# A two-layer graph attention kernel in float32: row loads in fewer, larger transfers, weight loads held back behind VectorE, and a new order at the end of a pass

## The chip, the core and the metric

The kernel runs on one core of a Trainium2 chip. The metric is the device time in microseconds (us) of one execution. The engines are named as the profile names them: PE (TensorE, matmuls) with PEld (its weight loads), DVE (VectorE), ACT (ScalarE), POOL (GpSimd) and SP (SyncE, which here only issues DMAs). Each engine works through its own instructions in order, and waits where a semaphore isn't there yet. All DMAs but two go through SP's one queue, in the order of the program.

## What is computed

There are 128 graphs of 64 nodes with 768 features. The features are normalised, and two layers of graph attention follow; the result is added to the input.

```python
h = jnp.maximum(_layernorm(x, axis=-1), 0.0)
for l in range(L):                               # L = 2
    m_left  = einsum('bsh,oh->bso', h, W_left[l])
    m_right = einsum('bsh,oh->bso', h, W_right[l])
    u_left  = einsum('bih,bjh->bij', h, m_left) / temper
    u_right = einsum('bih,bjh->bij', h, m_right) / temper
    u = u_left * adj_tri + u_left * diag_mask + u_right * swapaxes(adj_tri, 1, 2)
    delta_exp_u = exp(u) * adj
    attention = delta_exp_u / (sum(delta_exp_u, axis=2, keepdims=True) + 1e-10)
    h_lin = einsum('bsh,oh->bso', h, W_lin[l]) + b_lin[l]
    ctx = matmul(attention, h_lin)
    h = relu(_layer_norm(ctx, ln_a[l], ln_b[l]))
return x + h
```

All of it is float32.

## The kernel before

**Tiling and passes.** The tokens are cut into 16 blocks u = 0 to 15 of 8 graphs (512 tokens). Each layer has a pass one (`pass_one`: m_left, m_right, scores, softmax; the attention goes to DRAM) and a pass two (`pass_two`: h_lin, context, normalisation). Pass one takes two blocks at a time: a superblock U = 0 to 7, blocks 2U and 2U + 1.

**Products.** The two 768 x 768 projections of a superblock are done by a scheme of fast matrix multiplication: 29 products (`PRODUCTS`, `NP = 29`) of sums of weight blocks with sums of token blocks, each for the left and the right weights (k = 0, 1). A product writes one of the PSUM banks X, Y, Z (left) or V, right (right); each result is then read out (`read`, line 303) by ACT where an accumulator `m` is new, and added to `m` by DVE otherwise (line 221). One product is 16 matmuls, about 3.43 us. In layer 0's first superblock the weight sums are made as they are needed, on DVE and POOL, and stored to DRAM (`ws`); in all later superblocks they are streamed from there into a ring of eight buffers `wp` (`RINGS = 8`): the load for a product is issued when the product eight before it has released its buffer, about seven products (24 us) ahead.

**Slots.** The order of everything beside the matmuls is written out by hand. A superblock has 4 x 29 = 116 slots, and `run(slot)` is called four times in each product: slots 4i to 4i + 3 belong to product i. `put(slot, f)` lists work for a slot; slots with nothing listed take from the queue `idle`. A list given to `put_all` fills one slot after the other; `None` leaves one empty. What is put in a slot stands at that place in the queue of its engine, SP's included.

**Rows and blocks.** In layer 0, for each block from 2 on, `load_rows` reads the rows of x into SBUF; `transpose_rows` makes the statistics (line 338, DVE), normalises (ACT, line 399) and transposes on DVE (line 414); `store` writes the block to DRAM in four transfers (line 410); and `load_h` brings it back in the layout that the matmuls need (line 373). In `block(n, slot)` the store comes 6 slots after the last transpose, the next block's row load one slot later and `load_h` from 15 slots after the last transpose. The two blocks of a superblock start at the slots in `starts`. Layer 1 does the same from the rows that pass two of layer 0 wrote, without the statistics. A row load is 8 transfers; each takes one graph of 64 rows, as rows 0 to 31 and 32 to 63 side by side on 32 partitions. Blocks 0 and 1 of layer 0 are made by PE transposes in `first`, and lines 674 and 675 store them at slots 54 and 58 of superblock 0, for pass two.

**Held loads.** `HELD` lowers the number of weight loads that SP has issued by the end of a product near a superblock's border, so that other DMAs stand ahead of them in SP's queue. `paced(to, f)` (line 143) writes zeros to one column of a buffer on DVE before the load f into it is issued, so that the load waits for DVE's place.

**Scores.** `scores` (line 464, 192 short matmuls) runs within products 0 and 2 of the next superblock, for the two blocks of the one before, and at the end of pass one for blocks 14 and 15. The generator `chain` is the softmax of a block cut into steps: two with mask products on DVE (line 480), the add (484), the exponential on ACT (486), multiply and sum (488, 490), the division (492 to 494), then transpose (498) and eight stores. `softmax(u)` gives these 15 steps. At the end of pass one, lines 763 to 768 place those of blocks 14 and 15; what goes to `put_all` there runs in the first slots of pass two (two slots to each of its products). Pass two's first products are read out at line 303 by ACT and line 221 by DVE into `hl`.

Of the kernel before, what the change touches and what calls it, by code (L numbers as in the profile page):

```python
# [17 lines left out]
def kernel(  # L18
# [12 lines left out]
    nc = tc.nc  # L31
# [24 lines left out]
    NBB = T // S  # L56
    RINGS = 8
# [5 lines left out]
    none = [None]  # L63

    def put(slot, *fs):
        plan.setdefault(slot, []).extend(fs)

    def put_all(slot, fs, step=1):
        for f in fs:
            if f is not None:  # L70
                put(slot, f)
            slot += step
        return slot
# [50 lines left out]
    NP = len(PRODUCTS)  # L124
# [10 lines left out]
    RING = [wpool.tile([P, 2, K2, D], F32, name=f"wp{i}") for i in range(RINGS)]  # L135
# [4 lines left out]
    def room(n, m):  # L140
        return ROOM[:, n * K2 * D:(n + m) * K2 * D]

    def paced(to, f):

        nc.vector.memset(to, 0.0)
        f()
# [49 lines left out]
    def stream(l, n):  # L196
        nc.sync.dma_start(RING[n % RINGS], WS[l][n % NP])
# [34 lines left out]
    HT, TS = {}, {}  # L232
# [42 lines left out]
    def token_op(l, U, op, eng):  # L275
        i, o, sign, a, b = op
        t = new_ts((l, U, o))
        added(eng, t, sign, tokens(l, U, a), tokens(l, U, b))
        TS.setdefault((l, U), {})[o] = t

    AHEAD_X = 4
    SLOTS = 4 * NP

    def put_token_ops(l, U, part):

        count = {}
        for op in X_OPS:
            n = count[op[0]] = count.get(op[0], 0) + 1
            slot = 4 * (op[0] - AHEAD_X) + n - 1
            if (slot < 0) == (part == "before"):  # L290
                put(slot + (SLOTS if slot < 0 else 0), lambda op=op: token_op(l, U, op, nc.gpsimd))
# [20 lines left out]
    KEPT = [[dram.tile([P, C, T], F32, name=f"h{l}_{u}") for u in range(NB)] for l in range(L)]  # L312
    ROWS = [dram.tile([NBB, S, H], F32, name=f"z_{u}") for u in range(NB)]
# [41 lines left out]
    def blocks_tile(pool):  # L355
        if pool is not None:
            return pool.tile([P, H // 32, Q, 32], F32, name="xb", bufs=1)
        return room(6, 6).rearrange("p (b q j) -> p b q j", q=Q, j=32)

    def load_rows(l, u, pool=None):  # L360

        XR[l, u] = []
        for g in range(2):
            t = rows_tile(pool, g)
            for a in range(4):
                i = 4 * g + a
                src = x[u * NBB + i] if l == 0 else ROWS[u][i]
                nc.sync.dma_start(t[a * 32:(a + 1) * 32], src.rearrange("(k j) h -> j k h", k=2))
            XR[l, u].extend([t[:, 0, :], t[:, 1, :]])

    def load_h(which, l, u):
# [12 lines left out]
    def transpose_rows(l, u, pool=None):  # L384

        xr, todo = XR[l, u], []
        if l == 0:
            mv = stat.tile([P, Q, 2], F32, name="mv0", bufs=2)
            sd = stat.tile([P, Q], F32, name="sd0", bufs=2)
            rs = stat.tile([P, Q], F32, name="rs0", bufs=2)  # L390
            nb = stat.tile([P, Q], F32, name="nb0", bufs=2)

            def scale():
                nc.scalar.activation(sd, mv[:, :, 1], AF.Sqrt, bias=eps_in)
                nc.vector.reciprocal(rs, sd)
                nc.vector.scalar_tensor_tensor(nb, mv[:, :, 0], -1.0, rs, op0=ALU.mult, op1=ALU.mult)

            def norm(q):
                nc.scalar.activation(xr[q], xr[q], AF.Relu, bias=nb[:, q:q + 1], scale=rs[:, q:q + 1])

            norms = [lambda q=q: norm(q) for q in range(Q)]
            stats = [lambda q=q: mean_var(mv[:, q, :], [xr[q][:, :HH], xr[q][:, HH:]]) for q in range(Q)]
            for f in stats + none * (4 * (u < 4)) + [scale] + norms:
                todo.extend([f] + none * (u >= 4))
        xb = blocks_tile(pool)

        def store():
            to = KEPT[l][u].rearrange("(b i) c t -> i c b t", b=4)
            for a in range(4):
                nc.sync.dma_start(to[:, :, :, a * P:(a + 1) * P],  # L410
                                  xb[a * 32:(a + 1) * 32].rearrange("i (c b) q j -> i c b (q j)", b=4))

        for q in range(Q):
            todo.append(lambda q=q: nc.vector.transpose(
                xb[:, :, q, :], xr[q].rearrange("p (b j) -> p b j", j=32)))
            todo.extend(none * (l or u >= 4))
        todo.append(store)
        return todo
# [7 lines left out]
    def pass_one(l, aside):  # L426
        with (tc.tile_pool(name=f"ps_one{l}", bufs=1, space=bass.MemoryType.PSUM) as ps,
# [76 lines left out]
                        nc.sync.dma_start(to[a // 2, a % 2, g], at[a * 32:(a + 1) * 32, g])  # L504

            TURNS = {0: 0, 2: 1}
            HELD = {NP - 2: 1, NP - 1: 2, 0: 3, 1: 4}
            sent = [RINGS - 1 if l else NP + 5]

            def project(U, weights, done):  # L510
# [35 lines left out]
            def streamed(U):  # L546
                def done(i):
                    while sent[0] < min(U * NP + i + RINGS - HELD.get(i, 0), NU * NP):
                        stream(l, sent[0])
                        sent[0] += 1  # L550
                return (lambda i, k: RING[(U * NP + i) % RINGS][:, k]), done

            def first():
# [47 lines left out]
                hts = [new_ht() for _ in range(2)]  # L601
# [66 lines left out]
                for n, (s0, s1, s2, s3) in {4: (3, 4, 5, 8), 5: (6, 7, 8, 12), 6: (13, 14, 15, 19),  # L668
# [2 lines left out]
                    put(s1, lambda n=n: inverse(n))  # L671
                    put(s2, lambda n=n: norm(n))
                    put(s3, lambda n=n: turn(n), lambda n=n: settle(n))
                for n, slot in ((0, 54), (1, 58)):
                    put(slot, lambda n=n: nc.sync.dma_start(KEPT[0][n], hts[n]))
                put(3, lambda: load_rows(0, 2))
                count = {}
                for op in X_OPS:
                    n = count[op[0]] = count.get(op[0], 0) + 1
# [28 lines left out]
            for U in range(NU):  # L708
                if U:
                    weights, done = streamed(U)  # L710
                if l or U:
                    put_token_ops(l, U, "after")
                if U + 1 < NU:
                    def block(n, slot):
                        u = 2 * U + 2 + n
                        *todo, store = transpose_rows(l, u)
                        slot = put_all(slot, todo)
                        put(slot + 6, store)
                        if u + 1 < NB:
                            put(slot + 7, lambda: load_rows(l, u + 1))  # L720
                        slot = max(slot + 15, (92, 103)[n]) if U == 0 and l == 0 else slot + 15
                        put(slot, lambda: load_h(1, l, u))
                        if l:
                            put_all(slot + 20, affine(1, l, u))

                    if l:
                        starts = (6 if U else 20, 48)
                    else:
                        starts = (6, 52) if U else (26, 66)
                    for n, slot in enumerate(starts):  # L730
                        put(slot - 1, lambda n=n, slot=slot: block(n, slot))
                    if U:
                        for n in range(2):
                            steps = softmax(2 * U - 2 + n)
                            slot = put_all(20 + 40 * n if l else (34, 76)[n], steps[:6], 2)
                            slot = put_all(slot, steps[6:] + [lambda n=n: load_adj(2 * U + n)])
                            put(slot + 11, masked(2 * U + n))
                    else:
                        for n in range(2):
                            put((40 if l else 106) + 2 * n, masked(n))  # L740
                    put_token_ops(l, U + 1, "before")
                else:
                    for n in range(2):
                        put(12 + 28 * n, lambda n=n: load_h(2, l, n))
                        put_all(38 + 28 * n, affine(2, l, n))
                    for n in range(2):
                        steps = softmax(2 * U - 2 + n)
                        put_all(put_all(14 + 28 * n, steps[:6], 2), steps[6:])
                    put(40, lambda: load_adj(2 * U))
                    put(54, masked(2 * U))  # L750
                    put(SLOTS - 24, lambda: load_adj(2 * U + 1))
                    put(SLOTS - 10, masked(2 * U + 1))
                    put_sums_t((2, l, 0), 94, 2, 85)
                if U in aside:
                    aside[U]()
                project(U, weights, done)
                assert not plan, sorted(plan)
# [5 lines left out]
            scores(NB - 2, both[0])  # L763
            scores(NB - 1, ps_st.tile([P, 2 * TH], F32, name="Z"))
            one, two = softmax(NB - 2), softmax(NB - 1)
            for f in one[:2] + two[:2] + one[2:] + two[2:4]:
                f()
            put_all(2, two[4:])

    rows = {}  # L770

# [406 lines left out]
```

## Time and profile before

| | us |
|---|---|
| median of 3 runs | 2748.3 (2744.96 to 2752.83) |
| the profiled execution, its own time | 2748.58 |
| its span, first to last instruction | 2746.8 |
| granted TensorE clock | 0.994 |

Shares of 40 equal slices of the span (68.7 us each), each digit in tenths, for PE, DVE and the DMA engines:

```profile
PE   8899999999999999999999999999999999999998
...
DVE  7745755647557433334333645545446475676667
...
DMA  7967867768665334657586967868759524555655
```

The first 13 slices are pass one of layer 0, the next seven its pass two, slices 21 to 33 pass one of layer 1, and the rest its pass two. The DMA engines work hardest in the passes one. The largest DMA issues (count, KB each, median us from issue to landing):

```profile
wp<-ws SPq DMA_DIRECT2D x435, 512.0 KB, 5.4
ht<-h SPq DMA_DIRECT2D x62, 1536.0 KB, 8.8
h<-room SPq DMA_DIRECT2D x112, 384.0 KB, 6.2
...
room<-in_x_dram SPq DMA_DIRECT2D x112, 192.0 KB, 5.2
```

The first is the weight stream, the second `load_h`, the third the store of a block, the last the rows of layer 0 (layer 1's, from `z`, are as many).

### The profile page before, as it was taken

Reading aid. Unit: us, or ns where it says so; the run is one execution under the profiler, and the core shown is the slowest. Engines: PE = TensorE matmul, PEld = TensorE weight load, DVE = VectorE, ACT = ScalarE, POOL = GpSimd, SP = SyncE. Lnnn points to the kernel's source line nnn. Section 1 sums busy time; section 2 is a strip of 40 time slices with the busy share of each in tenths; the row PEclk is TensorE's granted clock in tenths of the full one; section 3 lists DMA queues with packets and bytes.
Section 4 is the critical chain, followed back from the end, with each engine's and each line's share of the span. In section 5 each row is a group of like instructions: output and inputs, shape, how many; then the busy total and the mean of one; then the engine's idle time right before and its main releaser. Section 6 shows DMA issues by size and latency. Waiting matters only on the chain.

```text
span 2746.8 us, 47294 instructions
## 1 busy us (share of the span) xinstructions
PE 2689.4 (98%) x18514; PEld 2309.1 (84%) x18514; DVE 1494.6 (54%) x2458; ACT 828.0 (30%) x1601; POOL 1380.5 (50%) x1071
## 2 busy tenths in 40 slices
PE   8899999999999999999999999999999999999998
PEld 7788888888888788888788888888888888888886
DVE  7745755647557433334333645545446475676667
ACT  4031231321310145445631221211212303444443
POOL 5534244333345766576343324335234185887886
PEclk9999999999999999999999999999999999999999
DMA  7967867768665334657586967868759524555655
GB/s 252 314 225 226 256 218 259 227 202 274 213 226 191 105 127 149 205 155 232 186 279 204 301 196 231 267 188 272 227 186 293 202 76 125 163 168 167 172 164 148
DMA packets 310222, 567.81 MB, mean 207 GB/s; under 512 B 62832, under 2 KB 190064, under 8 KB 301808
## 3 DMA queue, kind: packets, MB, share of 16 engines
q1 hardware_dynamic: 309840, 564.39, 64.7%
q8 instruction: 148, 2.42, 0.4%
q14 instruction: 74, 0.61, 0.1%
q10 hardware_dynamic: 160, 0.39, 0.0%
HBM read 429.40 MB, written 135.27 MB: 206 GB/s over the span
## 4 chain that ended last, share of the span: by engine, by line
PE 93%; POOL 2%; DVE 2%; issue 1%; DMA 1%; ACT 0%; DVEq 0%; POOLq 0%; ACTq 0%; SPq 0%
PE right L522 17%; PE X L1038 12%; PE X L522 10%; PE V L522 10%; PE Y L522 9%; PE Z L522 9%; PE V L1038 8%; PE Y L1038 6%; PE both L464 4%; PE Z L1038 4%; PE aux L846 2%; POOL room L221 1%; PE aux L869 1%; POOL ts L221 1%; PE Y L869 0%
## 5 line engine op out<-in xcount | busy, mean ns | idle before, releaser
L221 POOL TENSOR_TENSOR ts<-ht 128x512 f32<-128x512 f32 x352 | 478.7, 1366 | 176.5 <-PE X L1038 76.8
L221 POOL TENSOR_TENSOR ts<-ht,ts 128x512 f32<-128x512 f32 x192 | 253.2, 1327 | 386.4 <-PE V L522 232.7
L522 PE MATMUL right<-ts,wp 128*128 128x252 f32 (+1 forms) x1632 | 382.1, 377 | 0.0
L522 PEld LDWEIGHTS right<-ts,wp 128*128 128x128 f32 x1632 | 311.1, 191 | 39.1
L473 POOL TENSOR_TENSOR wm<-adj,tri 128x256 f32<-128x256 f32 x60 | 42.8, 736 | 433.0 <-DMA wp<-ws 285.4
L221 DVE TENSOR_TENSOR m<-m,X 128x512 f32<-128x512 f32 x160 | 105.5, 684 | 282.9 <-ACT m L303 199.8
L1038 PE MATMUL X<-room,ts 128*128 128x256 f32 x1024 | 247.2, 383 | 10.1 <-ACT hl L303 9.9
L221 DVE TENSOR_TENSOR m<-m,right 128x504 f32<-128x504 f32 (+1 forms) x304 | 199.2, 672 | 90.3 <-PE right L522 77.1
L522 PE MATMUL Z<-ts,wp 128*128 128x256 f32 x992 | 234.5, 379 | 0.0
L221 POOL TENSOR_TENSOR ts<-ht,ht 128x512 f32<-128x512 f32 x128 | 163.3, 1286 | 138.8 <-PE right L522 93.6
L1038 PEld LDWEIGHTS X<-room,ts 128*128 128x128 f32 x1024 | 193.3, 192 | 42.8 <-issue 12.5
L522 PE MATMUL X<-ts,wp 128*128 128x256 f32 x872 | 208.7, 382 | 1.0 <-DVE wp L221 1.0
L522 PEld LDWEIGHTS Z<-ts,wp 128*128 128x128 f32 x992 | 188.4, 190 | 24.9
L522 PE MATMUL V<-ts,wp 128*128 128x252 f32 (+1 forms) x864 | 201.6, 376 | 0.0
L303 ACT ACTIVATE m<-right 128x504 f32<-128x504 f32 (+1 forms) x64 | 36.1, 590 | 546.7 <-PE both L464 526.7
L522 PEld LDWEIGHTS X<-ts,wp 128*128 128x128 f32 x872 | 165.3, 191 | 24.9 <-issue 1.6
L1038 PE MATMUL Y<-room,ts 128*128 128x256 f32 x768 | 183.6, 381 | 0.0
L522 PEld LDWEIGHTS V<-ts,wp 128*128 128x128 f32 x864 | 164.2, 190 | 20.4
L380 ACT ACTIVATE ht<-ht,b_col,a_col 128x512 f32<-128x512 f32 x192 | 140.8, 803 | 112.6 <-DMA ht<-h 112.6
L1038 PEld LDWEIGHTS Y<-room,ts 128*128 128x128 f32 x768 | 146.9, 191 | 20.9 <-issue 0.6
L221 DVE TENSOR_TENSOR m<-m,Y 128x512 f32<-128x512 f32 x144 | 95.7, 683 | 118.6 <-PE Y L522 107.4
L221 DVE TENSOR_TENSOR hl<-hl,V 128x512 f32<-128x512 f32 (+1 forms) x136 | 89.0, 655 | 129.1 <-PE V L1038 121.5
(221 smaller groups left out, 4866.6 us busy)
## 6 DMA issues: line engine op xcount, KB each, us to landing
wp<-ws SPq DMA_DIRECT2D x435, 512.0 KB, 5.4
ht<-h SPq DMA_DIRECT2D x62, 1536.0 KB, 8.8
h<-room SPq DMA_DIRECT2D x112, 384.0 KB, 6.2
z<-z SPq DMA_DIRECT2D x128, 192.0 KB, 3.1
ws<-wp SPq DMA_DIRECT2D x93, 256.0 KB, 4.3
xr<-in_x_dram SPq DMA_DIRECT2D x120, 192.0 KB, 3.7
out_dram<-xr SPq DMA_DIRECT2D x120, 192.0 KB, 2.6
room<-in_x_dram SPq DMA_DIRECT2D x112, 192.0 KB, 5.2
```

Source lines behind the costliest of these rows:

```text
L221: (eng.tensor_add if sign == "+" else eng.tensor_sub)(o, a, b)
L303: nc.scalar.activation(to(o), p, AF.Copy, scale=1.0 if sign == "+" else -1.0)
L380: nc.scalar.activation(ht, ht, AF.Relu, bias=cols[1][:, c:c + 1], scale=cols[0][:, c:c + 1])
L464: nc.tensor.matmul(p[h * S + e:h * S + e + 32, q, e:e + 95], ht[:, c, b * S + e:b * S + e + 32], mb[:, e:e + 95], start=(c == 0), stop=(c ...
L473: nc.gpsimd.tensor_tensor(wm[:, :, k], adj[:, :, 1 - k], tri[:, k].unsqueeze(1).to_broadcast([P, Q, S]), op=ALU.mult)
L522: nc.tensor.matmul(p[:, g], wk[:, c, g * P:(g + 1) * P], tk[:, c, :].rearrange("p (b s) -> p b s", s=S)[:, :, :ns], start=(new and g == c ...
L846: nc.tensor.matmul(cx[k][i, m, :HH], at[j, q, :], hl[j, q, m * HH:(m + 1) * HH], start=True, stop=True)
L869: nc.tensor.matmul(parts[r, k][n][i], at[j, q, :], hl[j, q, cut], start=True, stop=True)
L1038: nc.tensor.matmul(p[:, n], b[t][:, c, r * P:(r + 1) * P], w[s][:, c, :], start=(i in FIRST and i not in PRELOAD and n == c == 0), stop=(c ...
```

## The change

It has five parts.

- `load_rows` issues 4 transfers in place of 8: for each half of the block (4 graphs) and each half k of the rows one transfer, to all 128 partitions.
- `HELD` is moved by one product. From superblock 1 on, the loads that are let go after product 3 are each tied to DVE by `paced`.
- The stores of blocks 0 and 1 leave superblock 0 and go to slots 20 and 26 of superblock 1.
- In layer 0 the starts move: from (26, 66) to (26, 62) in superblock 0, with two empty slots after the list of each of its blocks, and from (6, 52) to (8, 52) later. The second row load of superblock 0 goes to slot 112.
- At the end of pass one, block 14's add and exponential come before block 15's mask products, and all later steps of block 15 go to pass two's slots from 3 on.

```diff
@@ load_rows
             t = rows_tile(pool, g)
-            for a in range(4):
-                i = 4 * g + a
-                src = x[u * NBB + i] if l == 0 else ROWS[u][i]
-                nc.sync.dma_start(t[a * 32:(a + 1) * 32], src.rearrange("(k j) h -> j k h", k=2))
+            src = x[u * NBB + 4 * g:u * NBB + 4 * g + 4] if l == 0 else ROWS[u][4 * g:4 * g + 4]
+            for k in range(2):
+                nc.sync.dma_start(t[:, k, :], src[:, k * 32:(k + 1) * 32, :])
@@ transpose_rows
             for f in stats + none * (4 * (u < 4)) + [scale] + norms:
                 todo.extend([f] + none * (u >= 4))
+            todo.extend(none * (2 * (u < 4)))
@@ pass_one
-            HELD = {NP - 2: 1, NP - 1: 2, 0: 3, 1: 4}
+            HELD = {NP - 1: 1, 0: 2, 1: 3, 2: 4}
@@ streamed
                     while sent[0] < min(U * NP + i + RINGS - HELD.get(i, 0), NU * NP):
-                        stream(l, sent[0])
+                        if U and i == 3:
+                            paced(RING[sent[0] % RINGS][:, 0, 0, :1], lambda: stream(l, sent[0]))
+                        else:
+                            stream(l, sent[0])
                         sent[0] += 1
@@ first
-                for n, slot in ((0, 54), (1, 58)):
-                    put(slot, lambda n=n: nc.sync.dma_start(KEPT[0][n], hts[n]))
@@ pass_one, the loop over superblocks
+                if l == 0 and U == 1:
+                    for n in range(2):
+                        put(20 + 6 * n, lambda n=n: nc.sync.dma_start(KEPT[0][n], HT[1, 0, n]))
...
-                            put(slot + 7, lambda: load_rows(l, u + 1))
+                            put(SLOTS - 4 if U == 0 and l == 0 and n else slot + 7, lambda: load_rows(l, u + 1))
...
-                        starts = (6, 52) if U else (26, 66)
+                        starts = (8, 52) if U else (26, 62)
@@ pass_one, its end
             one, two = softmax(NB - 2), softmax(NB - 1)
-            for f in one[:2] + two[:2] + one[2:] + two[2:4]:
+            for f in one[:4] + two[:2] + one[4:]:
                 f()
-            put_all(2, two[4:])
+            put_all(3, two[2:])
```

## The prediction

> **What bounds the kernel now.** I read the page's busy line first, then the waits of PE, then the timeline at each wait, and last the DMA windows of an undisturbed superblock.
>
> ```profile
> PE 2689.4 (98%) x18514; PEld 2309.1 (84%) x18514; DVE 1494.6 (54%) x2458; ACT 828.0 (30%) x1601; POOL 1380.5 (50%) x1071
> ```
>
> PE is idle for 2746.8 - 2689.4 = 57.4 us. A change that leaves the matmuls alone can win no more than a part of that; it can lose without limit. PE's waits say where the idle time lies (total, times, longest, in us):
>
> ```profile
> PE both L464 <- issue: 13.0, 9, 2.8
> PE X L1038 <- ACT hl L303: 9.9, 2, 5.1
> PE Y L522 <- DMA wp<-ws: 6.3, 1, 6.3
> PE Y L522 <- DVE room L221: 3.4, 1, 3.4
> ```
>
> The second row is the start of pass two, once per layer; the third is the start of superblock 1 of layer 0. The timeline of each (start, duration, last the idle time before it):
>
> ```profile
> 919.39 0.38 DVE L484 TENSOR_TENSOR wp<-wp 128x256 f32<-128x256 f32 x1
> ...
> 919.81 0.42 ACT L486 ACTIVATE wp<-wp 128x256 f32<-128x256 f32 x1 [4.35 <-DVE wp L145]
> 920.13 0.58 ACT L303 ACTIVATE hl<-X 128x512 f32<-128x512 f32 x1
> ...
> 920.86 3.22 PE L1038 MATMUL X<-room,ts 128*128 128x256 f32 x8 [4.83 <-ACT hl L303]
> ```
> ```profile
> 132.41 3.75 PE L522 MATMUL Y<-ht,wp 128*128 128x256 f32 x8 [6.26 <-DMA wp<-ws]
> ```
>
> ACT's first eviction of pass two stands behind the last block's exponential, and that behind DVE's whole tail of the block before. In steady superblocks (108 us each) PE has no gap, so there only a loss is possible. What carries a steady superblock is the lead of its transfers. SP's queue around one row load, and the windows (share of the DMA engines, GB/s) for row loads and for weight loads:
>
> ```profile
> 392.53 5.20 SPq L410 DMA_DIRECT2D h<-room  x4
> 397.83 6.02 SPq L368 DMA_DIRECT2D room<-in_x_dram  x8
> 403.94 0.84 SPq L197 DMA_DIRECT2D wp<-ws  x2
> ```
> ```profile
> 402.50:406.50 4.00, 4.00 (x21) 3.54 (x20) 3.17 (x5) 1.75 (x4) 3.05 (x3) 1.00 0.96 263
> 408.50:410.50 2.00, 2.00 (x11) 1.78 (x10) 1.24 (x3) 0.00 (x0) 0.00 (x0) 1.00 1.04 411
> ```
>
> Per engine and busy time that is 263/16/0.96 = 17.1 GB/s for rows and 411/16/1.04 = 24.7 GB/s for weights.
>
> [...] In the kernel before the row load's source reads 32 x 2 x 768[...]. The new load's destination is 128 partitions, but its source is 4 blocks x 32 rows x 768[...].
>
> **Part by part.**
>
> *Row loads.* Per block 8 transfers of 192 KB become 4 of 384 KB. SP saves perhaps 3 us of its 6.02. The bytes (1.573 MB) take 1573/16/17.1 = 5.7 us on 16 engines, but on 4 engines 393 KB each: 15.9 us at 24.7 GB/s, 23.0 us at 17.1. [...] I take a value nearer the fast end, 17.6 us. Everything SP issues later queues behind this on these four engines. Steady case, product 10 of the superblock at 355: SP issues the load of product 16 at 395.4 (product 9 begins), the four stores of h to 401 (their packets last some 6.4 us: 1573 KB at the 244 GB/s of 396 to 401, so to about 403.7), then rows, then the load of product 17. Rows end at 421.3; that load adds 524 KB/16/24.7 = 1.3 us and about 1 us to land: 423.6. PE begins product 17 at 422.77. Stall 0.8 us; none (margin 0.9) at the fast end, 6.2 us at the slow end. The next loads have 3.43 us more each and catch up. 11 row loads of layer 0 and 13 of layer 1 stand so: 24 x 0.8 = 19 us, between 0 and 149. On DVE the statistics of the block (L338) wait for the same rows in layer 0; its eviction behind them is due at the same product 17, so this is not added again.
>
> *First superblock.* Two places. The rows of block 2 now sit for 17.6 us on four engines in front of the first stores of weights; weight sums write into buffers only after those stores have landed, first at slot 25 (product 6). Some 5 us. For block 3 the rows' slot goes from 50 to 52 and the statistics from 66 to 62, a lead of 10 slots of 0.86 us = 8.6 us against 13.7:
>
> ```profile
> 67.53 6.06 SPq L368 DMA_DIRECT2D room<-in_x_dram  x8
> ...
> 83.48 1.00 DVE L338 BATCH_NORM_STATS2 st<-room 128x6 f32<-128x384 f32 x2
> ```
>
> On 4 engines the last rows come near 70 + 17.6 + 2 = 90 us, the statistics' place on DVE is near 79: DVE, which PE's evictions and the weight sums stand behind, is held for about 10 us; some 8 reach PE. Together +13, between 0 (rows on 16 engines) and 25.
>
> *Stores of blocks 0 and 1 moved to superblock 1, last row load of superblock 0 at slot 112.* 3.1 MB, 8 us of all engines at 24.7 GB/s each, leave the busy stretch from 72 to 100 us, and 8 row loads no longer stand ahead of the weight stores that the first streamed loads wait for. That removes the 6.26 us stall and the slow first matmuls behind it (3.75 against 1.89): 8.1 us. The rows of block 4 then delay the loads of products 5 to 7, and the held loads wait on DVE behind that block's statistics: 0 to 5 us back. I take -5. In superblock 1 these stores lie in a stretch that in the superblock at 355 has 41% DMA use: nothing.
>
> *Held weight loads.* From superblock 1 on, five loads (products 6 to 10) wait for memsets on DVE at product 3. A memset takes 59 ns: 70 of them are 4 us in all, in an idle stretch of DVE (16.9 us idle after 362). Their slots come free at 352 to 370.6, DVE has finished the statistics at 362, product 6 begins at 385: 14 us for a transfer of about 5. Behind the memsets on DVE stand only the reciprocal and the next evictions, which wait for ACT until 378; on SP only the other held loads and, later, the stores and rows of slot 40 (20 in layer 1). Price 0. The holds may also quieten the DMA queues in the score matmuls (13.0 us of issue waits): between -10 and +10, taken as 0.
>
> *Order at the end of pass one.* Block 14's add and exponential go ahead of block 15's mask products; the rest of block 15 follows at slots 3 and on. ACT then evicts the first X at once, and PE's third product starts near 915.9. The next wait is ACT's exponential of block 15 in front of the eviction for the fifth product: DVE's tail of block 14 from 913.95 is 0.88+0.42+0.66+0.18+1.23+0.45 = 3.8, then memsets, an eviction and the add 1.7, exponential 0.5, eviction 0.6: 920.6 against 926.07 before. 5.4 us; by the same sum in layer 1 2268.2 against 2274.23, 6. Together -11 (bounds -8 and -15).
>
> **Sum.** -11 - 5 + 13 + 19 = +16 on the profiled execution's 2748.6 us (span 2746.8 and 1.8 around it; the median of the runs is 2748.3): 2765 us.
>
> **Rivals.**
>
> *A, 16 engines after all (the other side).* If the rows spread as before, they land in the 5.2 us that they take now and nothing stands behind them: -11 - 8.1 = -19, 2729 us. [...]
>
> *B, four engines, but hidden.* At the weights' 24.7 GB/s the steady margin is +0.9 us and the stalls vanish: -11 - 5 + 8 = -8, 2741 us, at the edge between faster and no change. Against it: rows ran at 17.1 in every window that I read.
>
> *C, four engines at 17.1 GB/s.* 24 x 6.2 = 149, with -11 - 5 + 20: about 2900 us. [...]
>
> My forecast and C are one mechanism, the place of the rows in four queues, and it decides from about 17 us of rows per block, where the 3 us that the other parts win are used up: below, the change is no slower.
>
> **How the numbers follow.** About 0.3%, 8 us, is what can be told from no change. Forecast (2750 to 2810) 0.45, A 0.22, B 0.22, C and what lies between 0.11. Faster: A whole and a third of B, 0.28; same: the rest of B and the low edge of the forecast, 0.16; slower 0.56. The range 2724 to 2825 takes in A's price and most of the forecast's tail; its own range is 2745 to 2825.
>
> **What would show it.** Row transfers that take about 15 to 23 us to land in place of 5 and DMA share well below 0.9 in their stretch [...]; waits of PE on weight loads at product 17 of layer 0 and product 12 of layer 1; DVE waiting for rows at L338; no wait on hl at the start of pass two; no 6.3 us wait at superblock 1. Row loads landing in 5 us would make the prediction wrong and A right.

## The result, and the profile after

The changed kernel takes 2956.1 us (median of 4 runs, 2953.8 to 2959.8) against 2749.6 us for the kernel before on the same chip. The ratio is 1.0754, with a 95% interval of 1.0734 to 1.0774. The forecast was 2765 us, its range ended at 2825: the direction was right, the size was not. The profiled execution took 2959.8 us, its span is 2958.0 us, 211.2 us longer than before.

The busy line of the page of the changed kernel (engine, us, share of the span, instructions):

```profile
PE 2740.9 (93%) x18514; PEld 2337.7 (79%) x18514; DVE 1510.4 (51%) x2528; ACT 828.9 (28%) x1601; POOL 1382.7 (47%) x1071
```

PE runs as many matmuls as before. Its idle time went from 57.4 to 217.1 us (+159.7), and its busy time rose by 51.5 us. Both need an explanation. The waits of PE (total, times, longest):

```profile
PE X L522 <- DMA wp<-ws: 75.8, 11, 13.4
PE Y L522 <- DMA wp<-ws: 65.6, 11, 10.1
PE Y L522 <- DVE m L221: 22.6, 3, 8.4
PE both L464 <- issue: 13.2, 8, 2.9
PE Z L522 <- DVE ht L221: 6.8, 1, 6.8
...
PE X L1042 <- ACT hl L303: 0.9, 2, 0.6
```

The wait on hl at the start of pass two is gone (9.9 before). The single wait of 6.3 us on streamed weights has become 22 waits with 141.4 us. Most of them stand at products 17 and 28 in layer 0 and at products 12 and 22 in layer 1; in the first superblock of layer 1 they are at products 7, 15 and 22. Three of the six waits at product 17 are put down to VectorE instead (the 22.6 us above). The windows of the DMA queues around the rows of one block in layer 1 (start and end, length, busy time of PE, PEld, DVE, ACT and POOL, the granted TensorE clock, the share of the 16 DMA engines, GB/s):

```profile
1798.00:1802.00 4.00, 4.00 (x21) 3.54 (x20) 3.34 (x8) 0.00 (x0) 3.84 (x4) 1.00 0.25 103
...
1804.00:1808.00 4.00, 4.00 (x21) 3.54 (x20) 1.75 (x3) 0.00 (x0) 0.00 (x0) 1.00 1.12 261
1808.00:1812.00 4.00, 0.79 (x4) 0.37 (x2) 0.68 (x1) 0.00 (x0) 0.00 (x0) 1.00 0.98 231
...
1814.00:1816.00 2.00, 0.00 (x0) 0.00 (x0) 0.00 (x0) 0.00 (x0) 0.00 (x0) 0.50 1.00 226
1816.00:1818.00 2.00, 0.00 (x0) 0.00 (x0) 0.00 (x0) 0.00 (x0) 0.00 (x0) 0.50 0.27 104
1818.00:1820.00 2.00, 0.10 (x1) 0.14 (x1) 0.00 (x0) 0.00 (x0) 0.00 (x0) 0.50 0.57 139
```

While rows are alone in the queues, 0.25 of the engines work: four of sixteen. The row window of the kernel before, which the prediction shows, had 0.96. The packets tell the same: the 512 of a block have 3.7 to 4.05 in work at a time and take 21.0 to 22.6 us from first to last in steady layer 1, and 18.3 to 21.2 in layer 0, where before they took about 8. The source's outermost size is 4 graphs here; in the kernel before it was 32 rows. That four engines follow from it was an assumption of the prediction, with no measurement behind it then; e6 and e7 vary that size.

The windows also show how rows reach the weights. SyncE's queue and PE there (start, duration; last the idle time before it):

```profile
1781.83 3.25 SPq L197 DMA_DIRECT2D wp<-ws  x5
1785.17 8.72 SPq L410 DMA_DIRECT2D h<-room  x4
1793.93 4.49 SPq L367 DMA_DIRECT2D room<-z  x4
1798.52 4.35 SPq L197 DMA_DIRECT2D wp<-ws  x2
1803.04 0.32 SPq L372 DMA_DIRECT2D ht<-h  x1
1803.41 3.83 SPq L197 DMA_DIRECT2D wp<-ws  x1
```
```profile
1819.89 3.75 PE L522 MATMUL X<-ts,wp 128*128 128x256 f32 x8 [11.11 <-DMA wp<-ws]
```

Two weight loads of 128 packets each, those of products 22 and 23, stand behind the rows. Of these 256 packets, 192 begin from 1802 to 1808, with twelve in work at a time. Then the load of ht runs there. No weight packet begins from 1807.3 to 1813.5; then follow 96 of the third load's 128. Only as the rows end (their last packet is through at 1818.1) do weight packets go on, 34 of them from 1817 to 1819 with four in work at a time: the missing quarter, on 4 of 16 engines. PE goes on with product 22 at 1819.89.

In layer 0 the same rows hold VectorE as well. DVE and PE at product 17 (DVE's last idle time in brackets):

```profile
451.04 1.02 DVE L338 BATCH_NORM_STATS2 st<-room 128x6 f32<-128x384 f32 x2 [2.86 <-DMA room<-in_x_dram]
...
456.58 1.02 DVE L338 BATCH_NORM_STATS2 st<-room 128x6 f32<-128x384 f32 x2 [4.28 <-DMA room<-in_x_dram]
457.64 0.21 DVE L339 BATCH_NORM_AGGREGATE mv<-st 128x2 f32<-128x12 f32 x1
459.55 0.18 DVE L394 RECIPROCAL rs<-sd 128x4 f32<-128x4 f32 x1 [1.70 <-ACT sd L393]
459.76 0.16 DVE L395 SCALAR_TENSOR_TENSOR nb<-mv,rs 128x4 f32<-128x4 f32 x1
459.84 0.68 DVE L221 TENSOR_TENSOR m<-m,Y 128x512 f32<-128x512 f32 x1
```
```profile
460.58 3.78 PE L522 MATMUL Y<-ht,wp 128*128 128x256 f32 x8 [7.13 <-DMA wp<-ws]
```

PE's wait is put down to a weight load, but that load's last packets are through near 458. PE goes on 0.06 us after DVE's add from bank Y ends (459.84 + 0.68 = 460.52). That add stands in DVE's order behind the reciprocal, the reciprocal waits for ACT's square root, and that for the statistics of rows whose last packet was through at 456.0. On ACT 1.28 us of this way are the load of a table before the square root (L393, at 457.93).

The 51.5 us of busy time are the stalls' echo: after a stall of several microseconds PE's first eight matmuls take 3.75 us in place of 1.89, and the clock column above has fallen to 0.50. After the waits of 3.7 us and over they took 3.50 to 3.78 us in this trace. After a wait of 2.04 us (superblock 1, product 28) the first group took 3.28 us. After waits of 1.0 to 2.0 us it takes 1.97 us at most, as here at the start of superblock 1, where the kernel before had waited for 6.26 us and then run at 3.75:

```profile
136.62 1.97 PE L522 MATMUL Y<-ht,wp 128*128 128x256 f32 x8 [1.13 <-DMA wp<-ws]
```

### The profile page after: what moved, and what is told of

It reads as the page before. It is cut to its first block, busy times and chain, and to the rows that moved or that the text cites. A ratio compares the mean times of both kernels' runs of the same rounds, so it can differ in the third digit from the quotient of the medians.

```text
span 2958.0 us, 47162 instructions
## 1 busy us (share of the span) xinstructions
PE 2740.9 (93%) x18514; PEld 2337.7 (79%) x18514; DVE 1510.4 (51%) x2528; ACT 828.9 (28%) x1601; POOL 1382.7 (47%) x1071
## 4 chain that ended last, share of the span: by engine, by line
PE 75%; DMA 17%; SPq 2%; DVE 2%; POOL 1%; issue 1%; ACT 0%; DVEq 0%; POOLq 0%; ACTq 0%
DMA wp<-ws 15%; PE right L522 11%; PE X L1042 11%; PE X L522 8%; PE V L522 7%; PE V L1042 7%; PE Y L522 7%; PE Z L522 6%; PE Y L1042 5%; PE both L464 4%; PE Z L1042 4%; PE aux L850 2%; DMA room<-in_x_dram 1%; DMA att<-wm 1%; PE aux L873 1%
## 5 line engine op out<-in xcount | busy, mean ns | idle before, releaser
L522 PE MATMUL X<-ts,wp 128*128 128x256 f32 x872 | 223.1, 402 | 77.6 <-DMA wp<-ws 75.8
L522 PEld LDWEIGHTS X<-ts,wp 128*128 128x128 f32 x872 | 172.3, 200 | 108.1 <-issue 78.0
L522 PE MATMUL Y<-ts,wp 128*128 128x256 f32 x608 | 156.1, 403 | 43.2 <-DMA wp<-ws 43.2
L522 PEld LDWEIGHTS Y<-ts,wp 128*128 128x128 f32 x608 | 122.5, 203 | 63.4 <-issue 45.8
```

Source lines behind the costliest of these rows:

```text
L522: nc.tensor.matmul(p[:, g], wk[:, c, g * P:(g + 1) * P], tk[:, c, :].rearrange("p (b s) -> p b s", s=S)[:, :, :ns], start=(new and g == c ...
```

## The experiments

T1 is the theory that the rows' confinement to four engines is the loss. T3, its rival, is that the held loads or the shifted starts are. The comparisons are with the kernel before on the same chip. Runs e1 to e4 share its runs (2749.0 us), as do e5 to e7 (2748.0), e8 to e10 (2749.2), e11 and e12 (2748.4); e13 has its own (2749.6).

### e1: the changed kernel with the old rows

```diff
-            for k in range(2):
-                nc.sync.dma_start(t[:, k, :], src[:, k * 32:(k + 1) * 32, :])
+            for a in range(4):
+                i = 4 * g + a
+                src = x[u * NBB + i] if l == 0 else ROWS[u][i]
+                nc.sync.dma_start(t[a * 32:(a + 1) * 32], src.rearrange("(k j) h -> j k h", k=2))
```

> The changed kernel with the row loads of the kernel before (8 transfers of 32 partitions, whose outermost size is 32). T1, the rows' confinement to four DMA engines is the whole loss: the sum of the other parts, -11 for the order at the end of pass one and -8 for the stores, gives about 2730 us, between 2725 and 2745, and no wait of PE over 3 us at product 17 of layer 0 or products 12 and 22 of layer 1. T3, the held loads on VectorE or the shifted starts cause it: above 2850 us, with the waits on wp still there.

Measured: 2728.9 us, ratio 0.9923 (0.991 to 0.9935). Its waits of PE:

```profile
PE both L465 <- issue: 11.2, 8, 2.9
...
PE X L1043 <- ACT hl L303: 1.4, 2, 0.9
...
PE Y L523 <- DMA wp<-ws: 1.1, 1, 1.1
```

One wait of 1.1 us on streamed weights is left. T3 falls. The other four parts together make the kernel faster, and the rows alone cost 2956.1 - 2728.9 = 227 us.

### e2: the kernel before with the new rows alone

The diff is that of e1, reversed.

> The kernel before with the new row loads alone (4 transfers of 128 partitions, source 4 x 32 x 768). T1: the whole loss and a little more, since the gains of the other parts are missing: about 2970 us, between 2935 and 2990, rows on about 4.0 engines for 17 to 21 us per block. T3: below 2790 us. If the parts hide each other's cost, something between: the kernel before has more stores ahead of the first streamed loads.

Measured: 2974.6 us, ratio 1.0832 (1.0811 to 1.0854): 225.6 us slower. So the rows cost the same in sum with or without the other parts, as T1 has it. The places differ: in e2 PE waits 15.9 us for weights at the start of superblock 1 (1.1 in the changed kernel), and in layer 0 it waits at product 16, put down to VectorE (five of six to the rows' statistics, L339), 4.3 to 6.2 us each.

### e3: the order at the end of pass one alone

```diff
-            for f in one[:2] + two[:2] + one[2:] + two[2:4]:
+            for f in one[:4] + two[:2] + one[4:]:
                 f()
-            put_all(2, two[4:])
+            put_all(3, two[2:])
```

> The kernel before with the new order at the end of pass one alone. As predicted: -11 us, 2738 us, between 2733 and 2741; PE's wait on hl falls from 9.9 us to about 1. If PE meets the next wait a little later: no change, 2749.

Measured: 2734.7 us, ratio 0.9949 (0.9935 to 0.9962), which is 10 to 18 us. PE's wait on hl:

```profile
PE X L1038 <- ACT hl L303: 1.7, 2, 1.0
```

It lost 8.2 us, and the rest of the gain is in the busy time (2684.3 against 2689.4 us). The step held.

### e4: the stores, the starts and the row load at slot 112

```diff
-                for n, slot in ((0, 54), (1, 58)):
-                    put(slot, lambda n=n: nc.sync.dma_start(KEPT[0][n], hts[n]))
+                if l == 0 and U == 1:
+                    for n in range(2):
+                        put(20 + 6 * n, lambda n=n: nc.sync.dma_start(KEPT[0][n], HT[1, 0, n]))
...
-                        starts = (6, 52) if U else (26, 66)
+                        starts = (8, 52) if U else (26, 62)
```

The two empty slots and the row load at slot 112 come with it, as in the change.

> The kernel before with the stores of blocks 0 and 1 in superblock 1, the last row load of superblock 0 at slot 112 and the shifted starts, rows as before. T1 and the prediction's term for 16 engines: -8 us, 2741, between 2738 and 2746, and the wait of 6.26 us at superblock 1 gone. T3 (the shifts are part of the loss): over 2760 us. Given back on the loads of products 5 to 7: 2746 to 2752.

Measured: 2747.0 us, ratio 0.9996 (0.9988 to 1.0004): no difference. Its waits of PE show why:

```profile
PE Z L523 <- DVE ht L221: 2.2, 1, 2.2
...
PE Y L523 <- DVE ht L186: 2.1, 1, 2.1
PE right L523 <- DVE m L221: 1.8, 2, 1.5
PE Y L523 <- DVE room L221: 1.7, 1, 1.7
PE Y L523 <- DMA wp<-ws: 1.7, 1, 1.7
PE right L523 <- DVE wp L221: 1.5, 1, 1.5
```

The wait of 6.3 us is down to 1.7, as predicted, but inside the first superblock PE now waits for VectorE in several places (2.2, 2.1, 1.8 and 1.5 us are new or longer). Its idle time is 58.4 us in all, against 57.4 before. Which of the shifts brings these waits was not separated.

### e5: the held loads alone

```diff
-            HELD = {NP - 2: 1, NP - 1: 2, 0: 3, 1: 4}
+            HELD = {NP - 1: 1, 0: 2, 1: 3, 2: 4}
...
-                        stream(l, sent[0])
+                        if U and i == 3:
+                            paced(RING[sent[0] % RINGS][:, 0, 0, :1], lambda: stream(l, sent[0]))
+                        else:
+                            stream(l, sent[0])
```

> The kernel before with the held loads alone (five weight loads behind memsets on VectorE at product 3, holds moved by one product). As predicted: no change, 2749 us, between 2744 and 2754. T3: slower by more than 50 us, with waits of PE on wp. Quieter DMA queues in the score matmuls: down to 2739, with the issue waits of PE below 13.0 us.

Measured: 2739.1 us, ratio 0.9965 (0.9952 to 0.9977), a gain of 6 to 13 us. The first two rows of PE's waits:

```profile
PE X L1041 <- ACT hl L303: 9.3, 2, 5.1
PE both L464 <- issue: 7.0, 6, 3.2
```

The score matmuls wait 7.0 us in place of 13.0: the branch of quieter queues, at its far end. That the queues are the reason is not shown. The waits are 7.1 us in e10 as well, but 11.2 in e1, which has the same held loads together with the moved stores and starts. T3 falls a second time.

### e6: rows of two graphs

```diff
-            for k in range(2):
-                nc.sync.dma_start(t[:, k, :], src[:, k * 32:(k + 1) * 32, :])
+            for a in range(0, 4, 2):
+                for k in range(2):
+                    nc.sync.dma_start(t[a * 32:(a + 2) * 32, k, :], src[a:a + 2, k * 32:(k + 1) * 32, :])
```

The diff is against the new row loads; the rest is the kernel before. These are eight transfers of 192 KB, as many and as large as its own.

> The kernel before with row loads of two graphs each: 8 transfers of 64 partitions, source 2 x 32 x 768, as many and as large as before. T1 (the outermost size sets the engines): two engines, 32 to 42 us per block, and well over the changed kernel: each block adds some 15 to 20 us more than with four engines, 24 blocks, so 3200 to 3450 us. If the size or the number of partitions of a transfer were what slowed the changed kernel, and not the outermost size: at or below 2790 us.

Measured: 3419.7 us, ratio 1.2438 (1.242 to 1.2455). A window with rows alone:

```profile
1984.00:1988.00 4.00, 4.00 (x20) 3.54 (x20) 2.50 (x5) 0.00 (x0) 2.24 (x2) 1.00 0.14 56
```

0.14 is two engines of sixteen. A block's packets take 33 to 39 us, 35.3 on average, against 21.1 in e2 (means over the same 21 blocks): 14.2 us more rows cost 3419.7 - 2974.6 = 445 us, 18.5 us for each of the 24 blocks, 1.3 us for each microsecond. T1 gave 3200 to 3450 us. So the outermost size decides, not number or size.

### e7: sixteen transfers of 32 partitions

```diff
             for k in range(2):
-                nc.sync.dma_start(t[:, k, :], src[:, k * 32:(k + 1) * 32, :])
+                for a in range(4):
+                    nc.sync.dma_start(t[a * 32:(a + 1) * 32, k, :], src[a, k * 32:(k + 1) * 32, :])
```

The diff is against the new row loads; the rest is the kernel before.

> The kernel before with 16 row loads of 32 partitions and one row each (96 KB, source 32 x 768): outermost size 32, packets of 3072 bytes as in the changed kernel. T1: all 16 engines and no loss but for SP, which issues twice as many: 2745 to 2765 us. If the order in which the rows are read (one row of each partition per transfer) was what slowed the changed kernel: above 2850 us.

Measured: 2754.3 us, ratio 1.002 (1.0014 to 1.0027). Twice as many transfers, each with one row per partition, cost 0.2% together. Outermost size 32 has no loss beyond that.

### e8 and e9: rows from GpSimd's queue

In both, `nc.sync` in `load_rows` becomes `nc.gpsimd`; e8 has the new rows, e9 the old.

> The changed kernel with its four row loads per block issued by GpSimd in place of SyncE: another DMA queue, and eight semaphores of its own, the same four engines and the same bytes. T1a, weight loads are late because they stand behind the rows in the same queue: most of the 210 us comes back, below 2830 us; what stays is VectorE's statistics of layer 0, which wait for the rows themselves. T1b, the four engines as such are too slow [...]: over 2900 us. What GpSimd loses by issuing is told by the next run.

> The control of the run before: the changed kernel with the old row loads (16 engines), issued by GpSimd. If issuing from GpSimd costs nothing: 2729 us as from SyncE. GpSimd is busy for half of the span, and behind a row load that waits for its buffers stand its sums of tokens and weights: up to 2780 us.

Measured: e8 2768.0 us (ratio 1.007, 1.0053 to 1.0087), e9 2741.6 (0.9971, 0.9958 to 0.9985). Moving the rows takes back 188 us, but not for the reason that was to be tested. A window of e8 with the rows of one block:

```profile
1653.00:1657.00 4.00, 4.00 (x21) 3.54 (x20) 1.52 (x3) 0.00 (x0) 3.79 (x4) 1.00 0.84 139
```

Row packets alone have 11.2 in work at a time there, against 3.7 to 4.05 from SyncE's queue. So the same four transfers are not confined to four engines from this queue; the reason is not shown. That window is a busy one: over a whole block the rows of steady layer 1 have 5.3 to 9.2 packets in work and take 14.3 to 19.5 us, not much less than on four. On the page of e8 a row load lands after 15.0 us (e9, half the size: 7.7). So e8 changes two things at once, the queue and the engines, and can't tell which of them takes the loss back. GpSimd's issuing costs 2741.6 - 2728.9 = 13 us.

### e10: the two parts that won

The kernel before with the diffs of e3 and e5.

> The kernel before with the two parts that won by themselves, the order at the end of pass one (0.9949) and the held loads (0.9965). If they add: 0.9914, 2725 us. If the held loads and the stores together were what the first run's 0.9923 held: the same as that within 0.2%.

Measured: 2728.7 us, ratio 0.9926 (0.9914 to 0.9939). The gains add but for 3 us, which is within the intervals, and the stores bring nothing on top: e1 and e10 agree. In the traces e1 wins 5.2 us over e10 on streamed weights (1.1 against 6.3) and gives 4.1 back in the score matmuls (11.2 against 7.1). These two are the fastest versions that were run, some 20 us faster than the kernel before.

### e11 and e12: rows from ScalarE's queue

As e8 and e9, with `nc.scalar`. In the trace the loads that SyncE issues name eight semaphores in turn, and SyncE waits on a load that was issued earlier before it reuses its semaphore.

> The changed kernel with its four row loads per block issued by ScalarE: a DMA queue of its own, but in the program as built these loads take their places in the same rotation of eight semaphores as SyncE's, so that SyncE must still wait for a row load to land before it reuses its semaphore. Ring theory, the weights are late because their descriptors stand behind the rows in SyncE's queue on four engines: the control of the next run plus about 26 us. Rotation theory, SyncE itself is held up by the semaphores of the rows: more than 100 us over the control, and SyncE's waits on row loads (190 us in the changed kernel) still there.

> The control of the run before: the changed kernel with the old row loads (16 engines) issued by ScalarE. ScalarE is busy for 28 per cent of the span; behind a row load that waits for its buffers or for a semaphore stand its evictions, so up to 40 us over the 2729 us of the first run; 2729 to 2770 us.

Measured: e11 2909.5 us (ratio 1.058, 1.0556 to 1.0603), e12 2755.1 (1.0024, 1.0015 to 1.0032): 154 us over the control, not 26. Two of SyncE's waits in e11:

```profile
SPq L504 <- DMA room<-in_x_dram: 101.9, 22, 7.4
SPq L197 <- DMA room<-z: 100.6, 17, 7.8
```

By the letter the rotation theory won: a queue of its own does not free the weights. But the rows still have only 2.5 to 3.7 packets in work at a time here, as on four engines. This pair cannot tell whether the weights were late through shared engines or through SyncE.

### e13: eight transfers on the same four engines

```diff
             for k in range(2):
-                nc.sync.dma_start(t[:, k, :], src[:, k * 32:(k + 1) * 32, :])
+                for e in range(2):
+                    nc.sync.dma_start(t[:, k, e * HH:(e + 1) * HH], src[:, k * 32:(k + 1) * 32, e * HH:(e + 1) * HH])
```

> The changed kernel with each row load cut into two by half rows: 8 transfers of 192 KB, outermost size still 4, the same bytes on the same four engines, but eight in place of four of the semaphores in rotation held by rows. Queue theory, a weight load is late because a quarter of its packets stands behind the rows on four engines: the changed kernel's 2956 us plus what the shorter packets (1536 bytes) add to the time of a block, about 24 times that. Rotation theory, SyncE cannot issue the weight loads: all of them after the rows are held, so well above that, over 3050 us even where a block's rows take no longer than the 17 to 21 us of the changed kernel.

Measured: 2905.5 us, ratio 1.0573 (1.0555 to 1.059): 51 us faster than the changed kernel. A window with rows alone still shows four engines:

```profile
1761.00:1765.00 4.00, 4.00 (x20) 3.54 (x19) 3.04 (x6) 0.00 (x0) 3.84 (x4) 1.00 0.27 100
```

A block's rows take 18.9 us in place of 20.8 (means over the same 21 blocks), about 2 us less; 24 times that is close to the 51 us. SyncE's waits on rows did not grow with the doubled semaphores, as rotation theory has it, but fell from 207 to 153 us (57 in e1). So this run alone doesn't rule the rotation out. The single stalls do, where PE waits for weights. In steady superblocks of the changed kernel, e2, e6 and e13, SyncE had issued the load that PE waited for 11 to 24 us before PE went on, so issuing was not late. PE went on 1.7 to 2.2 us after the rows' last packet, whether the rows took 18 us or 38 (products 12 and 22 of layer 1, 28 of layer 0). What bounds there is the time that rows hold the four engines. When the rows start against PE can still hang on SyncE's waits. In e11 the rotation may still carry part of the 154 us; that stays open.

## Why the prediction was wrong

The profiled execution is compared with e1's, whose span is 2727.1 us, 230.9 us shorter. Superblocks are taken from the first matmul of one to that of the next.

| step | predicted | measured |
|---|---|---|
| order at the end of pass one | -11 (-8 to -15) | -14, interval -10 to -18 (e3) |
| stores, starts, slot 112 | -5 | -1, interval -3 to +1 (e4, with 16 engines) |
| held loads | 0 (-10 to +10) | -10, interval -6 to -13 (e5) |
| rows in the first superblock | +13 | +7.4 (125.7 us against e1's 118.3) |
| steady row loads | +19 (0 to 149) | +223: +76 in layer 0, +147 in layer 1 |

The measured column adds up to +205; the medians differ by 206.5.

*Right.* Four engines for the rows, with a source of outermost size 4 (share 0.25); the first place of each superblock (product 17 in layer 0, product 12 in layer 1; products 28 and 22 were not named); DVE waiting for rows at L338; the wait on hl; the stall at superblock 1; nothing in pass two (584.3 us from superblock 7 of layer 0 to layer 1, against 584.5).

*The step that failed* is "24 x 0.8 = 19 us". The mechanism stands. The term of one block was mis-sized, in four ways that the trace shows:

1. The rows' own time. I took 17.6 us a block, an estimate nearer the faster of two measured rates. Measured: 21.0 us at product 17, 21.7 at the second place in layer 1. An engine moves 393 KB in that, 18.7 and 18.1 GB/s, near the slow end of 17.1 that the row window before had shown. That is +3.4 to +4.1 us each, and there was no slack left to take it in. The packets show what one figure for the rate had missed. With rows alone the window from 1798 gives 103/16/0.25 = 25.8 GB/s an engine, as fast as the fast end, and a row packet of layer 1 takes 127 ns. With the other twelve engines at work it takes 205 ns, 15.0 GB/s, slower than the slow end (layer 0: 133 and 188 ns). The weights and ht behind the rows keep those twelve busy for more than half of the time in layer 1, and with them at work the rows did not reach the fast end. Why the rows slow down then is open.
2. What follows the rows in layer 0. "So this is not added again" took the statistics as parallel to the weight load. Both start from the rows' end, but DVE's way is longer: 4.6 us from the rows' last packet (455.98) over the end of the add (460.52) to PE (460.58), against the 2.3 us that I gave the weight load. With the margin of 18.52 us from the rows' first packet (434.93) to the time when PE was due (453.45), 21.05 + 4.60 - 18.52 = 7.13 us, the measured wait. Mine was 17.6 + 2.3 - 19.1 = 0.8.
3. "11 row loads of layer 0 and 13 of layer 1 stand so" took one margin for all. At product 12 of layer 1 it is also 18.6 us (rows 1749.8, PE due 1768.35), and 21.0 + 1.8 - 18.6 = 4.2 is the wait (4.25 in the trace). At the second place it was 18.5 us before (rows 1768.25, product 22 at 1786.72) but is 12.3 now (1796.5, due 1808.8): 21.7 + 1.8 - 12.3 = 11.2, where 11.1 was measured. The rows start 6 us later against PE. The view of SyncE above shows five weight loads and the stores of h ahead of them, 8.72 us for the four stores. The kernel before has 5.44 there:

```profile
1759.93 5.44 SPq L410 DMA_DIRECT2D h<-room  x4
1765.41 6.40 SPq L368 DMA_DIRECT2D room<-z  x8
```

   I read this as the first stall's pile-up, as weight loads that had been behind are then issued together. No run took the first stall away alone, and its length doesn't set the margin: it is 12.2 us at this place in e6, with a first stall of 18.6 us, and 12.6 in e13, with one of 2.4. What these three kernels share is that SyncE itself waits between the two row loads for the first rows to land before it issues more: 8.8 us here, 7.9 in e6, 8.4 in e13, but 1.8 in the kernel before. So the rotation may well be what delays the second rows; that stays open. My sentence "the next loads have 3.43 us more each and catch up" looked only at the weights.
4. Each stall's echo. PE's busy time is 56.5 us above e1's. The 3.75 us after a stall were in a fence of the prediction, and I charged them at superblock 1 only.

The rival C, 24 x 6.2 = 149 us, had the rows' time nearly right (23.0 us) and still fell short, for want of points 2 to 4. It had only part of a chance of 0.11 because the faster end looked likelier than what had been measured in place.

*Rival A* came out at 2729, and e1, with sixteen engines, measures 2728.9. This is luck in the terms: the order gave 3 us more, the held loads 10 us that I priced at nothing, and the stores nothing of their 8.

*Rival B* needed rows of 15.9 us. That is about what they would take alone (1573 KB at 103 GB/s: 15.3 us, an estimate), but in the stream of weights a block took 18.3 to 22.6 us in steady superblocks. Its threshold was sound where PE waits for weights: with 18.5 us of margin and 1.8 us behind the rows, the stall begins at some 16.7 us of rows, near the 17 of the prediction. At product 17 of layer 0, with 4.6 us behind the rows, it begins near 13.9 us, so rows of 15.9 us would not have been hidden there. Both figures are estimates from the margins above.

## What to carry to other kernels

Look at the outermost size of a transfer's source before counting partitions: from SyncE's queue, rows with 128 partitions at the destination and a first size of 4 in the source kept 0.25 of the engines busy, with 64 partitions and 2 it was 0.14. Behind such rows the weight loads, which have to arrive whole, came late (22 waits, 141.4 us), so price such a transfer by its tail: in these runs a wait for weights was the rows' time plus 1.7 to 2.2 us, less the margin from the rows' first packet to the time when PE was due. Do it for each place with that place's own margin, DVE work behind it and the slow matmuls after a stall (3.75 us for eight in place of 1.89). Take the rate of a few engines with the others at work (205 ns for a row packet of layer 1), not alone (127 ns), and ask what the first stall does to the next.

## What the runs showed of the hardware

- The DMA share with rows alone was 0.25 for an outermost size of 4 and 0.14 for 2, from SyncE's queue. Rows from GpSimd's queue with outermost size 4 had 11.2 packets in work at a time in one window, 5.3 to 9.2 over a block of steady layer 1.
- On four engines a row packet of 3072 bytes took 127 to 133 ns with nothing else in work, and 188 to 205 ns with eleven to thirteen other packets in work.
- In the traces of seven kernels (before, after, e1, e2, e6, e11, e13) PE's first eight matmuls of a product half took 1.97 us at most after waits of 1.0 to 2.0 us (the very first product apart), and 3.09 us or more after waits of 3.7 us and over. Between 2.0 and 3.7 us both occur.
- Cutting a row into halves at the same four engines made a block faster: packets of 1536 bytes took 72 ns in layer 0 and 76 in layer 1, those of 3072 bytes 149 and 169. Why is open.
- With five weight loads tied to a later point of the superblock the issue waits of the score matmuls fell from 13.0 to 7.0 us and the time by 0.35%, for the same work (e5). With the stores and starts moved too they were 11.2 us (e1).
